# A state-space layer with experts on one core: first projections from centred input, finer layer-norm steps, and two products between two sets of transposes

## The chip, the cores and the metric

The kernel runs on one core of a Trainium2 chip. The metric is device time in microseconds of one execution; the median of several runs is given. Five engines work side by side, each with its own instruction stream in order: TensorE (PE, with weight loads as PEld), VectorE (DVE), ScalarE (ACT), GpSimd (POOL), and SyncE (SP), whose queue issues all DMAs here. [...]

## The reference, cut to what matters

One sequence of L = 2048 tokens with 1024 channels, all float32. The input is layer-normed; the normed input goes to a Mamba-2 style layer and to a base projection with low-rank experts; both results are added to the input.

```
xn    = (x - mean(x)) / sqrt(var(x) + 1e-5)               # over 1024 channels
proj  = xn @ in_proj_w.T                                  # gate 4096 | x 4096, B 1024, C 1024 | dt 64
xBC   = silu(causal_conv4(proj[x,B,C]) + conv_bias)
dt    = softplus(proj[dt] + dt_bias);  dA = exp(dt * -exp(A_log))
state = state * dA + (dt * x) outer B;  y = state @ C     # per token, 64 heads, 8 groups
y     = y + D * x;  yn = rmsnorm_per_group(y) * norm_weight * silu(gate)
attn  = yn @ out_proj_w.T
ffn   = xn @ W_base.T + b_base + lora(top-2 of 8 experts of rank 16, from xn)
out   = x + attn + ffn
```

## The kernel before, in words

Channels lie on partitions, tokens along the free axis. The sequence is cut into two halves `s` of 1024 tokens (`TS`), each into two blocks of 512 (`TB`), each into chunks of 128 (`Q`).

**The large products** are done in pairs of 128-row weight tiles by a seven-product scheme (`pair`). A product is four matmuls of 128x512 in the program, which the trace shows as eight records. Products go round PSUM tiles `pa`, `px`, `py` of the pool `ps_proj`. The seven left operands are four weight quarters `a11, a12, a21, a22` loaded by DMA and four sums `s1..s4` made on GpSimd (line 395) and stored to DRAM for the second half (line 397). The loads of the left operands are issued in the order a11, a21, a22, store of s1, store of s2, a12, store of s3, store of s4. The seven right operands `ops_of["x", s]` are the normed input's quarters `b11, b21, b22` and four differences (`t1, t2, t4`, and `b22 - b12` in the place of b12). Within a pair DVE adds `s16` (line 448) and `s15` (line 452) out of PSUM, and evicts two of the four results with an addition (line 494); ACT copies `s1` (line 444) and evicts another with an activation (line 492). Product 7 goes into the same PSUM tile as product 6 and must wait until s16 has read it; product 4 likewise waits until the eviction after product 7.

**The first pair** cannot use differences that do not exist yet, so `plain_pair` does its four results straight: each is eight matmuls of 128x512 of weights by normed quarters, evicted by ACT.

**A start in pieces.** The first half is layer-normed in four pieces of 256 tokens (`ln_first`): mean over channels by matmuls with ones, subtraction on DVE, squares on ACT, variance by matmuls with ones, square root on ACT, reciprocal and multiplication on DVE into the operands. `small_first` then makes dt, router and low-rank products (`sm`) of two 128-token chunks a time. The order on PE is written out by hand from line 850 on: variances of pieces 0 and 1, `small_first(0)`, the mean of piece 2, `small_first(1)`, the mean of piece 3, and then the products of the plain pair with the rest between them.

**The main loop** goes over 32 blocks (half, group, block of 512) and in each over four chunks `c`: one such step is called a slot here. A slot takes `n` products from the stream (4 or 5, from a plan of due numbers), and between them the work of the scan: `scan_b` of this chunk (`ps_y`, `ps_e`, `ps_st`), and `scan_a` of the following one in three steps: (1) DVE scans the decays into `es` (line 673); (2) PE multiplies B by C and transposes B into one PSUM bank, "aux" (`ps_cb`), ACT copies both out (`cbm` line 683, `bt` line 685), DVE multiplies `es` by `cbm` into `dab` (line 687); (3) PE transposes x into the same bank (`ps_xt`), ACT scales it into `xdt` (line 698), GpSimd makes `xdd` (line 704). The bank has one buffer, so `ps_xt` has to wait for the copy `bt`. The root mean square of a finished block (`ps_nv`, evicted at line 797) uses that bank too, in slot c = 0.

```python
            products(1, parts[1])
            products(1, parts[2])
            next(a, None)          # step 2: B by C, transpose of B
            products(1, parts[3])
            next(a, None)          # step 3: transposes of x
```

`parts` holds side steps: the next block's convolution (`conv`, slots c = 1 and 2), gating of the block before (`norm_gate`, c = 0), squares (`norm_squares`, c = 3), and pieces of the small chain (`small`). In blocks 2, 5, 8 and 11 there is also `ln_next`, which norms a piece of the second half for its operands; the stages of those pieces stand in slots c = 1, 2 and 3, and in the block that follows come the steps of `small` for it. PE's order is as written; a scheduler orders the other engines' instructions when the kernel is built.

**The end** is the output projection, again in pairs, with accumulation in SBUF.

Of the kernel before, what the change touches and what calls it, by code (L numbers as in the profile page):

```python
# [27 lines left out]
P = 128  # L28
# [14 lines left out]
def mamba_lora_kernel(  # L43
# [125 lines left out]
    def over_channels(of, bank, name):  # L169
        ps = ps_one.tile([P, 2 * Q], F32, tag=bank, name=f"ps_{name}")  # L170
        for k, part in enumerate(of):
            mm(ps, ones, part, start=(k == 0), stop=(k == len(of) - 1))
        return ps

    def ln_first(i):


        flat = piece_of[0, i].rearrange("p k n q -> p k (n q)")
        bank = ("aux", "y", "e", "st")[i]
        if i < 2:  # L180
            of = [flat[:, k, :] for k in range(KT)]
        else:
            of = halved(flat, f"0_{i}")
        ps = over_channels(of, bank, f"mean_0_{i}")
        mean = p2.tile([P, 2 * Q], F32, tag="state", name=f"mean_0_{i}")
        nc.scalar.activation(mean, ps, AF.Copy, scale=1.0 / DM)
        sqs = []
        for h in range(2):
            normal(flat[:, 4 * h : 4 * h + 4, :], mean, ALU.subtract)
            for k in (4 * h, 4 * h + 2):  # L190
                sq = ev.tile([P, 2, 2 * Q], F32, tag="ev", name=f"lsq_0_{i}_{k}")
                nc.scalar.activation(sq, flat[:, k : k + 2, :], AF.Square)
                sqs.append(sq)
        if i < 2:
            of = [sqs[k // 2][:, k % 2, :] for k in range(KT)]
        else:
            of = pairs_sum(sqs)
        yield
        ps = over_channels(of, bank, f"var_0_{i}")
        std = p1.tile([P, 2 * Q], F32, tag="xdd", name=f"std_0_{i}")  # L200
        nc.scalar.activation(std, ps, AF.Sqrt, bias=eps, scale=1.0 / DM)
        nc.vector.reciprocal(std, std)
        cols = slice((i % 2) * 2 * Q, (i % 2 + 1) * 2 * Q)
        for h, j in enumerate((0, 1) if i < 2 else (6, 2)):
            normal(flat[:, 4 * h : 4 * h + 4, :], std, ALU.mult, ops_of["x", 0][j][:, :, cols])
        yield

    def first_sums():


        b11, b21, b22, t4, t1, t2, b12 = ops_of["x", 0]
        nc.vector.tensor_tensor(t1, b12, b11, ALU.subtract)
        nc.vector.tensor_tensor(t2, b22, t1, ALU.subtract)
        nc.vector.tensor_tensor(t4, b21, t2, ALU.subtract)
        yield
        nc.vector.tensor_tensor(b12, b22, b12, ALU.subtract)
        yield

    def ln_next(s, i):

        t = piece_of[s, i]
        flat = t.rearrange("p k n q -> p k (n q)")

        of = halved(flat, f"{s}_{i}")
        yield
        ps = over_channels(of, "st", f"mean_{s}_{i}")
        mean = p2.tile([P, 2 * Q], F32, tag="lnst", name=f"mean_{s}_{i}")
        nc.scalar.activation(mean, ps, AF.Copy, scale=1.0 / DM)
        yield
        sqs = []  # L230
        for h in range(2):
            normal(flat[:, 4 * h : 4 * h + 4, :], mean, ALU.subtract)
            for k in (4 * h, 4 * h + 2):
                sq = ev.tile([P, 2, 2 * Q], F32, tag="ev", name=f"lsq_{s}_{i}_{k}")
                nc.scalar.activation(sq, flat[:, k : k + 2, :], AF.Square)
                sqs.append(sq)
        of = pairs_sum(sqs)
        yield
        ps = over_channels(of, "st", f"var_{s}_{i}")
        std = p2.tile([P, 2 * Q], F32, tag="lnst", name=f"std_{s}_{i}")  # L240
        nc.scalar.activation(std, ps, AF.Sqrt, bias=eps, scale=1.0 / DM)
        nc.vector.reciprocal(std, std)
        for h in range(2):
            normal(flat[:, 4 * h : 4 * h + 4, :], std, ALU.mult)
        yield
        b11, b12 = t[:, 0:KH, 0, :], t[:, 0:KH, 1, :]
        b21, b22 = t[:, KH:KT, 0, :], t[:, KH:KT, 1, :]
        cols = slice(i * Q, (i + 1) * Q)
        t4, t1, t2, t3 = (
            ev.tile([P, KH, Q], F32, tag="ev", name=f"t_{s}_{i}_{j}") for j in range(4)  # L250
        )
        nc.vector.tensor_tensor(t1, b12, b11, ALU.subtract)
        nc.vector.tensor_tensor(t2, b22, t1, ALU.subtract)
        nc.vector.tensor_tensor(t4, b21, t2, ALU.subtract)
        nc.vector.tensor_tensor(t3, b22, b12, ALU.subtract)
        for j, src in enumerate((b11, b21, b22, t4, t1, t2, t3)):
            nc.sync.dma_start(xop_d[j][:, :, cols], src)
        yield
# [205 lines left out]
        quarter(1, 0, px, s1)  # L464
        yield

    def plain_pair(key, name, quarters, ops, quarter):


        t = left_operands(key, quarters, True)  # L470
        w = [t[i] for i in ("a11", "a12", "a21", "a22")]
        yield
        b11, b21, b22, _, _, _, b12 = ops()
        for n, (lo, hi) in enumerate(((b11, b21), (b12, b22))):
            for m in range(2):
                ps = ps_proj.tile([P, TB], F32, tag="proj", name=f"ps_p_{name}")
                for h, b in enumerate((lo, hi)):
                    for k in range(KH):
                        mm(
                            ps, w[2 * m + h][:, k, :], b[:, k, :],  # L480
                            start=(h + k == 0), stop=(h + k == KH), skip_group_check=True,
                        )
                quarter(m, n, ps, None)
                yield

    def stored(to, first_tile, s, func):


        def quarter(m, n, ps, add):
            e = ev.tile([P, TB], F32, tag="ev", name="ev")  # L490
            if add is None:
                nc.scalar.activation(e, ps, func)
            else:
                nc.vector.tensor_tensor(e, ps, add, ALU.add)  # L494
                if func != AF.Copy:
                    nc.scalar.activation(e, e, func)
            at = s * TS + n * TB
            nc.sync.dma_start(to[:, first_tile + m, at : at + TB], e)

        return quarter  # L500
# [24 lines left out]
    def in_pairs():  # L525
        for s in range(NS):
            ops = lambda s=s: ops_of["x", s]
            for g in range(G):
                if s and g == 0:
                    load_ops(s)  # L530
                for q, (i0, i1) in enumerate(((0, 1), (2, 3), (4, 5))):
                    tis = [4 * g + i if i < 4 else 32 + 8 * (i - 4) + g for i in (i0, i1)]
                    args = (
                        f"x{g}_{q}", f"x_{s}_{g}_{q}", halves(*(w_in[32 + t] for t in tis)), ops,
                        stored(raw_d[g], i0, s, AF.Copy),
                    )
                    yield pair(*args, s == 0) if s + g + q else plain_pair(*args)
                for q in range(2):
                    t = 4 * g + 2 * q
                    yield pair(  # L540
                        f"g{g}_{q}", f"g_{s}_{g}_{q}", halves(w_in[t], w_in[t + 1]), ops,
                        stored(gate_d[g], 2 * q, s, AF.Silu), s == 0,
                    )
            for q in range(4):
                yield pair(
                    f"b{q}", f"b_{s}_{q}", halves(w_base[2 * q], w_base[2 * q + 1]), ops,
                    stored(base_d, 2 * q, s, AF.Copy), s == 0,
                )
# [298 lines left out]
    next(lns[1])  # L847
    next(lns[0])
    next(lns[1])
    small_first(0)  # L850
    next(lns[2])
    small_first(1)
    next(lns[3])
    next(lns[2])
    next(stream)
    next(lns[3])
    next(stream)
    small_first(2)
    small_first(3)
    op_sums = first_sums()  # L860
    next(op_sums)
    next(stream)
    next(stream)
    next(op_sums)
    home = {
        "dtp": (p2, "xdt"), "u": (p2, "ecp"), "u2": (p2, "ecp"), "po": (p2, "xdt"),
        "at": (p2, "ecp"), "ex": (p1, "xdd"), "da": (p1, "es"), "run": (p2, "dab"),
# [35 lines left out]
    for b, blk in enumerate(blocks):  # L903
# [8 lines left out]
        for c in range(NQ):  # L912
# [8 lines left out]
                load_piece(*piece, "sg", p1)  # L921
                ln = ln_next(*piece)
            if after == 0 and c == 2:
                next(ln)
            if after == 0 and c == 3:
                side += steps(ln, 1)
            if after == 1 and c in (0, 2, 3):
                side += steps(rest, 1)
            if c in (1, 2) and nxt:
# [19 lines left out]
            if c == NQ - 1:  # L949
                sq = norm_squares(*blk)  # L950
                parts[1] += steps(sq, 2)
                parts[2] += steps(sq, 1)
            products(1, parts[1])
            products(1, parts[2])
            next(a, None)
            products(1, parts[3])
            next(a, None)
            if after == 0 and c in (1, 2):
                next(ln)
            for i in range(4, n):  # L960
                products(1, parts[i])

            if after == 0 and c == 1:
                next(ln)
# [153 lines left out]
```

## Time and profile before

| what | value |
|---|---|
| median of 3 runs | 3573.68 us (3573.0 to 3574.63) |
| the profiled execution's own time | 3579.01 us |
| its span, first to last instruction | 3577.2 us |
| PE busy | 3514.0 us (98%) |
| DVE, ACT, POOL busy | 2322.4, 943.7, 685.6 us |
| mean granted TensorE clock | 0.995 |

The span is 1.8 us short of that execution's time. The execution lay 5.3 us above the median of the runs. A row of the timeline has: start, duration, engine, line, operation, output and inputs, shapes, how many were merged, and in brackets the idle time before it and who ended it. A row of the windows has the stretch, its length, the busy time of PE, PEld, DVE, ACT and POOL (with numbers of instructions), the granted clock, the DMA share and GB/s. A row of the waits has the waiting operation, what it waited for, the sum in us, how many times, and the longest.

### The profile page before, as it was taken

The page shows a single profiled execution, that of the slowest core. Times are in us where ns is not written, and L with a number is a line of the kernel's source. Part 1 is how long each engine was busy: PE and PEld are TensorE (multiplying, and loading weights), DVE is VectorE, ACT ScalarE, POOL GpSimd, SP SyncE. Part 2 cuts the span into 40 slices and gives each one's busy share as a digit, 9 for nine tenths or more (in the row PEclk, how much of TensorE's full clock was granted, in tenths as well). Part 3 has the DMA queues.
Part 4 walks back from the last instruction along what each step waited for, and adds up shares of the span by engine and source line. Part 5 has one row for each costly group of instructions (what it writes and reads, how often), then busy time and mean ns, then how long its engine had stood idle before and what let it go on. Part 6 is the DMA issues. An engine that isn't in the chain of part 4 may idle for free. (4 is left out here: it accounts for less than half of the span.)

```text
span 3577.2 us, 36348 instructions
## 1 busy us (share of the span) xinstructions
PE 3514.0 (98%) x12370; PEld 1731.0 (48%) x12370; DVE 2322.4 (65%) x2713; ACT 943.7 (26%) x2170; POOL 685.6 (19%) x503
## 2 busy tenths in 40 slices
PE   8999999999999999999999999999999999999999
PEld 6444444544544444455455455455455444444444
DVE  6537877877877777676766777766776544434432
ACT  2213343333333333233333333333332100000000
POOL 2223323333323322011111111111112202220000
PEclk9999999999999999999999999999999999999999
DMA  3546565656555567656565555565656564455432
GB/s 124 183 154 205 187 199 186 193 191 197 179 189 185 182 195 244 207 191 189 182 195 176 184 184 194 180 192 183 184 188 208 207 209 160 135 165 196 151 112 88
DMA packets 394681, 648.60 MB, mean 181 GB/s; under 512 B 33024, under 2 KB 129408, under 8 KB 393600
## 3 DMA queue, kind: packets, MB, share of 16 engines
q1 hardware_dynamic: 394496, 646.27, 55.9%
q8 instruction: 99, 1.62, 0.2%
q14 instruction: 86, 0.70, 0.1%
HBM read 433.28 MB, written 212.86 MB: 181 GB/s over the span
## 5 line engine op out<-in xcount | busy, mean ns | idle before, releaser
L673 DVE TENSOR_TENSOR_SCAN es<-dab,here 128x1024 f32<-128x1024 f32 x128 | 304.9, 2382 | 347.0 <-POOL xdd L704 342.8
L704 POOL TENSOR_TENSOR xdd<-xdt,es 128x512 f32<-128x512 f32 x128 | 143.9, 1124 | 1212.1 <-ACT xdt L698 1005.6
L76 PE MATMUL ps_x_x<-op,s_x 128*128 128x512 f32 x752 | 340.7, 596 | 0.0
L76 PE MATMUL ps_y_x<-op,s_x 128*128 128x512 f32 x752 | 338.8, 593 | 0.0
L76 PE MATMUL ps_a_x<-op,a_x 128*128 128x512 f32 x752 | 338.1, 592 | 0.0
L632 DVE SCALAR_TENSOR_TENSOR xg<-rawx,cw,xg 128x512 f32<-128x512 f32 x384 | 295.4, 815 | 13.7 <-ACT xg L626 12.7
L698 ACT ACTIVATE xdt<-ps_xt,dt 128x64 f32<-128x64 f32 x1024 | 225.2, 331 | 189.3 <-PE ps_xt L79 187.5
L76 PE MATMUL ps_y_g<-op,s_g 128*128 128x512 f32 x512 | 232.0, 596 | 1.6 <-DVE s_g L452 1.6
L76 PE MATMUL ps_x_g<-op,s_g 128*128 128x512 f32 x512 | 231.8, 596 | 0.0
L76 PE MATMUL ps_x_o<-yop,s_o 128*128 128x512 f32 x512 | 230.2, 592 | 1.1 <-DVE s_o L448 1.1
L76 PE MATMUL ps_a_o<-yop,a_o 128*128 128x512 f32 x512 | 230.3, 592 | 0.0
L76 PE MATMUL ps_a_g<-op,a_g 128*128 128x512 f32 x512 | 230.2, 592 | 0.0
L76 PE MATMUL ps_y_o<-yop,s_o 128*128 128x512 f32 x512 | 230.2, 592 | 0.0
L76 PEld LDWEIGHTS ps_a_x<-op,a_x 128*128 128x128 f32 x752 | 140.3, 190 | 162.8 <-issue 162.1
L76 PEld LDWEIGHTS ps_x_x<-op,s_x 128*128 128x128 f32 x752 | 140.7, 191 | 161.4 <-issue 160.4
L757 POOL TENSOR_TENSOR state<-state,tot 128x512 f32<-128x512 f32 x112 | 159.3, 1423 | 304.6 <-PE ps_e L76 280.4
L76 PEld LDWEIGHTS ps_y_x<-op,s_x 128*128 128x128 f32 x752 | 139.2, 190 | 157.5 <-issue 155.0
L444 ACT COPY s_o<-ps_a_o 128x512 f32<-128x512 f32 x32 | 18.8, 586 | 707.5 <-PE ps_a_o L76 627.3
L687 DVE TENSOR_TENSOR dab<-es,cbm 128x1024 f32<-128x1024 f32 x128 | 164.2, 1283 | 30.3 <-ACT cbm L683 29.7
L76 PE MATMUL ps_x_x<-op,a_x 128*128 128x512 f32 x376 | 171.3, 599 | 9.2 <-DVE ev L494 9.1
L632 DVE SCALAR_TENSOR_TENSOR bc<-rawb,cw,bc 128x512 f32<-128x512 f32 x192 | 163.5, 884 | 12.7 <-ACT bc L626 12.4
L76 PEld LDWEIGHTS ps_y<-dab,xdt 128*64 128x64 f32 x2048 | 117.8, 136 | 102.3 <-issue 56.1
(213 smaller groups left out, 5030.0 us busy)
## 6 DMA issues: line engine op xcount, KB each, us to landing
dab<-da_d SPq DMA_DIRECT2D x128, 512.0 KB, 4.8
raw<-ev SPq DMA_DIRECT2D x192, 256.0 KB, 2.8
a_x<-in_w_in_dram SPq DMA_DIRECT2D x168, 256.0 KB, 3.4
ecp<-run_d SPq DMA_DIRECT2D x256, 128.0 KB, 3.6
gate<-ev SPq DMA_DIRECT2D x128, 256.0 KB, 3.0
sg<-gate SPq DMA_DIRECT2D x32, 1024.0 KB, 6.1
y<-xg SPq DMA_DIRECT2D x64, 512.0 KB, 3.6
yop<-y SPq DMA_DIRECT2D x32, 1024.0 KB, 6.2
```

The source lines that it names most:

```text
L76: tc.keep_in_program_order(nc.tensor.matmul(*args, **kw))
L444: nc.scalar.copy(s1, pa)
L632: nc.vector.scalar_tensor_tensor(dst[:, i, :], raw[:, i, k : k + TB], cw[:, ti, k : k + 1], dst[:, i, :], ALU.mult, ALU.add,)
L673: nc.vector.tensor_tensor_scan(es.rearrange("p h t -> p (h t)"), dab.rearrange("p h t -> p (h t)"), here, 0.0, ALU.mult, ALU.add,)
L687: nc.vector.tensor_tensor(ms, es, cbm.unsqueeze(1).to_broadcast([P, HG, Q]), ALU.mult)
L698: nc.scalar.activation(xdt[:, h, :], x_t[:, h, :], AF.Copy, scale=dt_of[s][:, half * NQ + c, at : at + 1],)
L704: nc.gpsimd.tensor_tensor(xdd, xdt, es[:, :, Q - 1 : Q].to_broadcast([P, HG, HP]), ALU.mult)
L757: nc.gpsimd.tensor_tensor(s3, s3, tot_of[s][:, half * NQ + c, hs].unsqueeze(2).to_broadcast([P, HG, HP]), ALU.mult,)
```

## The change

Three parts. In the start, `plain_pair` takes the centred pieces (x minus its mean) in place of the normed operands, a piece of 256 tokens at a time, so that a result is sixteen matmuls of 128x256; DVE multiplies by 1/sqrt(var+eps) (`rstd`) as it evicts. Its first two products stand right after the variances of pieces 0 and 1, each followed by the mean of piece 2 or 3; the small products come after them, and the four differences of the operands are made in one go. In `ln_next`, the work is cut into more steps, and these are spread over the slots: centring and squares move from ahead of slot c = 2 into its side steps, the variance to the end of that slot, the multiplications into slot c = 3. In every slot, step 2 of `scan_a` moves ahead of one more product, so that two products stand between it and the transposes of x.

```diff
 def ln_first(i):
-        std = p1.tile([P, 2 * Q], F32, tag="xdd", name=f"std_0_{i}")
+        cols = slice((i % 2) * 2 * Q, (i % 2 + 1) * 2 * Q)
+        if i % 2 == 0:
+            rstd_of[i // 2] = p2.tile([P, TB], F32, tag="xdt", name=f"rstd_{i // 2}")
+        std = rstd_of[i // 2][:, cols]
         nc.scalar.activation(std, ps, AF.Sqrt, bias=eps, scale=1.0 / DM)
         nc.vector.reciprocal(std, std)
...
 def first_sums():
         nc.vector.tensor_tensor(t4, b21, t2, ALU.subtract)
-        yield
         nc.vector.tensor_tensor(b12, b22, b12, ALU.subtract)
-        yield
...
 def ln_next(s, i):
                 sqs.append(sq)
-        of = pairs_sum(sqs)
-        yield
-        ps = over_channels(of, "st", f"var_{s}_{i}")
+            nc.vector.tensor_tensor(sqs[2 * h], sqs[2 * h], sqs[2 * h + 1], ALU.add)
+            if h:
+                nc.vector.tensor_tensor(sqs[0], sqs[0], sqs[2], ALU.add)
+            yield
+        ps = over_channels([sqs[0][:, 0, :], sqs[0][:, 1, :]], "st", f"var_{s}_{i}")
...
         nc.vector.reciprocal(std, std)
+        yield
         for h in range(2):
             normal(flat[:, 4 * h : 4 * h + 4, :], std, ALU.mult)
-        yield
+            yield
...
         nc.vector.tensor_tensor(t2, b22, t1, ALU.subtract)
+        yield
         nc.vector.tensor_tensor(t4, b21, t2, ALU.subtract)
...
-    def plain_pair(key, name, quarters, ops, quarter):
+    def plain_pair(key, name, quarters, quarter):
         t = left_operands(key, quarters, True)
-        w = [t[i] for i in ("a11", "a12", "a21", "a22")]
-        yield
-        b11, b21, b22, _, _, _, b12 = ops()
-        for n, (lo, hi) in enumerate(((b11, b21), (b12, b22))):
+        yield
+        for n in range(2):
             for m in range(2):
-                ps = ps_proj.tile([P, TB], F32, tag="proj", name=f"ps_p_{name}")
-                for h, b in enumerate((lo, hi)):
-                    for k in range(KH):
+                ps = ps_proj.tile([P, 2, 2 * Q], F32, tag="proj", name=f"ps_p_{name}")
+                for i in range(2):
+                    x = piece_of[0, 2 * n + i].rearrange("p k n q -> p k (n q)")
+                    for k in range(KT):
+                        w = t[f"a{m + 1}{k // KH + 1}"]
                         mm(
-                            ps, w[2 * m + h][:, k, :], b[:, k, :],
-                            start=(h + k == 0), stop=(h + k == KH), skip_group_check=True,
+                            ps[:, i, :], w[:, k % KH, :], x[:, k, :],
+                            start=(i + k == 0), stop=(k == KT - 1), skip_group_check=True,
                         )
-                quarter(m, n, ps, None)
+                quarter(m, n, ps.rearrange("p a t -> p (a t)"), rstd_of[n], ALU.mult)
...
 the written-out start:
     next(lns[1])
+    next(stream)
+    next(lns[2])
+    next(stream)
+    next(lns[3])
     small_first(0)
     next(lns[2])
     small_first(1)
     next(lns[3])
-    next(lns[2])
-    next(stream)
-    next(lns[3])
     next(stream)
     small_first(2)
+    next(stream)
     small_first(3)
-    op_sums = first_sums()
-    next(op_sums)
-    next(stream)
-    next(stream)
-    next(op_sums)
+    first_sums()
...
 the main loop:
             if after == 0 and c == 2:
-                next(ln)
+                side += steps(ln, 2)
             if after == 0 and c == 3:
-                side += steps(ln, 1)
+                side += steps(ln, 4)
...
             products(1, parts[1])
+            next(a, None)
             products(1, parts[2])
-            next(a, None)
             products(1, parts[3])
             next(a, None)
-            if after == 0 and c in (1, 2):
+            if after == 0 and c == 1:
                 next(ln)
             for i in range(4, n):
                 products(1, parts[i])
+            if after == 0 and c == 2:
+                next(ln)
```

More of the change, by code (lines that the diff above doesn't have):

```diff
@@ L173, in over_channels @@
         return ps
+    rstd_of = {}
     def ln_first(i):
@@ L199, in ln_first @@
         ps = over_channels(of, bank, f"var_0_{i}")
-        std = p1.tile([P, 2 * Q], F32, tag="xdd", name=f"std_0_{i}")
+        cols = slice((i % 2) * 2 * Q, (i % 2 + 1) * 2 * Q)
+        if i % 2 == 0:
+            rstd_of[i // 2] = p2.tile([P, TB], F32, tag="xdt", name=f"rstd_{i // 2}")
+        std = rstd_of[i // 2][:, cols]
         nc.scalar.activation(std, ps, AF.Sqrt, bias=eps, scale=1.0 / DM)
         nc.vector.reciprocal(std, std)
-        cols = slice((i % 2) * 2 * Q, (i % 2 + 1) * 2 * Q)
         for h, j in enumerate((0, 1) if i < 2 else (6, 2)):
@@ L465, in pair, with quarter @@
         yield
-    def plain_pair(key, name, quarters, ops, quarter):
+    def plain_pair(key, name, quarters, quarter):
         t = left_operands(key, quarters, True)
-        w = [t[i] for i in ("a11", "a12", "a21", "a22")]
         yield
-        b11, b21, b22, _, _, _, b12 = ops()
-        for n, (lo, hi) in enumerate(((b11, b21), (b12, b22))):
+        for n in range(2):
             for m in range(2):
-                ps = ps_proj.tile([P, TB], F32, tag="proj", name=f"ps_p_{name}")
-                for h, b in enumerate((lo, hi)):
-                    for k in range(KH):
-                        mm(
-                            ps, w[2 * m + h][:, k, :], b[:, k, :],
-                            start=(h + k == 0), stop=(h + k == KH), skip_group_check=True,
+                ps = ps_proj.tile([P, 2, 2 * Q], F32, tag="proj", name=f"ps_p_{name}")
[3 more added lines that the diff above has]
+                        w = t[f"a{m + 1}{k // KH + 1}"]
+                        mm(
+                            ps[:, i, :], w[:, k % KH, :], x[:, k, :],
+                            start=(i + k == 0), stop=(k == KT - 1), skip_group_check=True,
                         )
-                quarter(m, n, ps, None)
+                quarter(m, n, ps.rearrange("p a t -> p (a t)"), rstd_of[n], ALU.mult)
                 yield
     def stored(to, first_tile, s, func):
-        def quarter(m, n, ps, add):
+        def quarter(m, n, ps, add, alu=ALU.add):
             e = ev.tile([P, TB], F32, tag="ev", name="ev")
@@ L493, in quarter @@
             else:
-                nc.vector.tensor_tensor(e, ps, add, ALU.add)
+                nc.vector.tensor_tensor(e, ps, add, alu)
                 if func != AF.Copy:
@@ L532, in in_pairs @@
                     tis = [4 * g + i if i < 4 else 32 + 8 * (i - 4) + g for i in (i0, i1)]
[L533 to L537, printed above, removed]
+                    key, name = f"x{g}_{q}", f"x_{s}_{g}_{q}"
+                    quarters = halves(*(w_in[32 + t] for t in tis))
+                    to = stored(raw_d[g], i0, s, AF.Copy)
+                    if s + g + q:
+                        yield pair(key, name, quarters, ops, to, s == 0)
+                    else:
+                        yield plain_pair(key, name, quarters, to)
                 for q in range(2):
```

## The prediction, made before the changed kernel was run

> **What bounds the kernel now.** I read the page first: PE is busy 3514.0 us of a span of 3577.2, so all that can be won without removing matmuls is 63 us of gaps, and what a slow clock adds to the matmuls. Then the windows by stage, to see where the gaps lie, and the waits of PE, to see who ends them.
>
> ```profile
> 0.00:92.00 92.00, 75.67 (x274) 55.21 (x275) 60.13 (x69) 24.68 (x44) 19.49 (x33) 0.93 0.37 123
> 400.00:1320.00 920.00, 887.81 (x3403) 449.38 (x3402) 710.29 (x880) 325.57 (x727) 270.46 (x193) 0.99 0.59 191
> 1320.00:2400.00 1080.00, 1077.57 (x4264) 540.41 (x4263) 761.28 (x867) 361.92 (x866) 155.84 (x113) 1.00 0.60 192
> ...
> PE ps_xt L79 <- ACT bt L685: 14.7, 7, 5.5
> PE ps_x_g L76 <- DVE ev L494: 9.5, 4, 4.5
> PE ps_x_x L76 <- DVE ev L494: 9.1, 4, 4.8
> PE ps_sm L76 <- ACT std L201: 6.6, 1, 6.6
> PE ps_mean L76 <- DVE half L166: 4.7, 1, 4.7
> ```
>
> The start lacks 16.3 us of PE, the stretch with the second half's layer-norm pieces and their small chains (400 to 1320) lacks 32.2, all the rest 14.7. Each part of the change aims at one row of the waits. Then the timeline of the start, PE, SP and POOL:
>
> ```profile
> 13.74 7.07 PE L76 MATMUL ps_var<-lsq,ones 128*128 128x256 f32 x32
> 27.43 8.35 PE L76 MATMUL ps_sm<-wsm,op 128*128 128x200 f32 x32 [6.62 <-ACT std L201]
> 47.43 2.05 PE L76 MATMUL ps_mean<-half,ones 128*128 128x256 f32 x4 [4.70 <-DVE half L166]
> 91.32 3.60 PE L76 MATMUL ps_a_x<-op,a_x 128*128 128x512 f32 x8
> ...
> 17.77 1.28 SPq L391 DMA_DIRECT2D a_x<-in_w_in_dram  x3
> 27.05 0.42 SPq L391 DMA_DIRECT2D a_x<-in_w_in_dram  x1
> ...
> 30.25 1.30 POOL L395 TENSOR_TENSOR s_x<-a_x,s_x 128x512 f32<-128x512 f32 x1 [1.82 <-DMA a_x<-in_w_in_dram]
> ```
>
> The reader is to see that the quarter a12 of the first pair is issued only at 27.05, behind the stores of s1 and s2, which wait for GpSimd, and lands at 30.25.
>
> **Part 1, the start.** The work of PE hardly changes: four products of 32 records at 0.221 us (the variances: 7.07 / 32) are 7.07 us each, against 6.87 before (13.90 us for two, less overlap). Weights take 0.19 us a record and stay hidden. DVE gains four evictions of 0.68 us, ACT loses four of 0.60. The question is when each can run, so I walk it in the new order.
>
> Variances end at 20.8. a11 lands at about 21.2 (17.77 plus the median 3.4 from issue to landing); four matmuls with it take 1.7 us; the next needs a12. PE then stands from 22.9 to 30.25: the gap that ended at 27.43 now ends 2.8 us later. The clock is granted in steps of 3.4 us, and after such a gap at half speed:
>
> ```profile
> 28.00:32.00 4.00, 4.00 (x14) 4.00 (x13) 3.97 (x3) 0.00 (x0) 1.72 (x2) 0.50 0.71 221
> 170.00:172.00 2.00, 2.00 (x4) 0.83 (x3) 2.00 (x3) 0.00 (x0) 0.53 (x1) 0.50 0.66 245
> ```
>
> Twelve more matmuls take 5.2 us, or 8.2 with some 6 us at half speed: 38.4. DVE's queue has the eviction of this product ahead of the three sums for the mean of piece 2 (0.7 + 2.0 us), so PE waits to 41.5 for that mean (0.9 us), then does the second product to 49.3. Again eviction and three sums: PE waits to 52.3 for the mean of piece 3. From there nothing is late: that mean (0.9), four pairs of small products (10.99 us for two pairs, so 22.0), variances 2 and 3 (0.9 each) and two products (13.8) come to 38.5, so the second pair starts at about 90.8, and at 92.5 if the gap before 52.3 also halves the clock for one step. Before: 91.32. Behind it, the small chain on DVE starts with the second pair instead of at 78.14, after the fourth difference (2.29 us). It held DVE for 22 us; now s16, s15 and the eviction after product 7 stand inside it. That eviction is about 21 to 23 us behind the pair's start, and product 4 wants it after 6 x 3.43 = 20.6: 0.2 to 2.4 us of waiting. The chain's result is due on PE 27 us after that start and is ready at about 25. So the start is worth 92.5 - 91.3 and about 1 us of that wait, **+2 us (slower)**, with bounds of -5 (no half speed, no DVE wait) and +5. SP's stores of the four results move with them, ahead of a store and loads for the third pair, which is not due for 24 us; POOL's sums keep their place.
>
> [...] But the row 170 to 172 shows half speed after a gap of only 2.15 us (with another of 1.65 us some 4 us before it). [...] I take the row.
>
> **Part 3, two products before the transposes of x.** The worst of the seven waits:
>
> ```profile
> 1024.72 3.60 PE L76 MATMUL ps_a_x<-op,a_x 128*128 128x512 f32 x8
> 1031.05 0.68 DVE L448 TENSOR_TENSOR s_x<-ps_x_x,s_x 128x512 f32<-128x512 f32 x1
> 1032.42 1.06 ACT L638 ACTIVATE xg<-xg 128x1024 f32<-128x1024 f32 x1 [5.31 <-DVE xg L632]
> 1033.53 0.27 ACT L685 COPY bt<-ps_cb 128x128 f32<-128x128 f32 x1
> 1033.85 1.11 PE L79 MATMUL ps_xt<-ident,xg 128*128 128x128 f32 x4 [5.53 <-ACT bt L685]
> ```
>
> ACT stands in the convolution's silu, which waits for DVE; bt is behind it. In the new order bt is ahead of that silu. But what is late next is s16 on DVE, for product 7: with the same DVE work ahead of it, it ends at about 1032.4, so PE resumes then instead of 1034.76: 2.3 won, not 5.5. So went through all: at 582.71 0.85 (next product needs only ACT's copy); at 933.36 0.4 of 1.03 (s15, behind the moved dab of 1.23); at 1207.13 1.4; at 1251.12 about 1.1 of 3.01 (one of two squares of the norm still ahead of bt); at 1281.60 nothing of 2.28, since DVE has no gap from 1276 to 1304 and PE waits for it at 1303.48 anyway; at 199.09 nothing (that scan is written without products between). Sum 6.1. Half-speed steps fall away for about 2.5 us (one of two at 1033, half of one at 1251).
>
> It also adds waits. dab (1.23 us, 128 times) now stands ahead of the eviction of one more product, and B by C asks for the bank one product earlier: against the root mean square's eviction that leaves -1.2 us at 556.8, -0.4 at 1000.3 and 0.5 or more elsewhere. Bank 1.6; at 1007.60 0.5; other evictions I put at 1.5. The trace before cannot show those: bounds 0 and 8. After 1320 PE waits 2.4 us in 1080, so DVE's slack is the cover there; were it gone, each slot would cost up to 1.2.
>
> **Part 2, finer layer-norm.** DVE's 14 us a piece stay; slot c = 2 loses some 4.5 us of it and c = 3 gains it. But the eight waits for ev lie mostly in the block after a piece, where the small chain, the gating (reciprocal 3.35, product 2.29) and the convolution meet. At 473.73 (4.54) DVE is held by the gate's DMA, whose buffer is the piece's, freed as late as before. The wait at 755.98 (4.77) shrinks, since the new order puts ev behind three convolution steps, not six (3 x 0.74 = 2.2), and with it one half-speed step (1.7): 3.9 won. I cost the rest at nothing, bounds -5 and +3; the seven stores a piece keep their place.
>
> **Sum.** +2.0 - 6.1 - 2.5 - 3.9 + 1.6 + 0.5 + 1.5 = -6.9 us. Made against the profiled execution (3579.0), taken over to the median of the runs: 3573.7 - 6.9 = **3567**.
>
> **The rivals.** (a) *All the waits go.* For it: the releaser in each row is just what the change moves. Against it: DVE's next piece of work is late by nearly as much. It would give 14.1 (transposes) + 6.4 (half-speed steps at 1033, 1251, 1282) and 5 in the start: 3548. (b) *DVE in order becomes the bound: slower.* The moved dab holds the eviction of the second product by 1.23 us in each of some 60 slots of the first half. It decides once those evictions have less than 1.23 us to spare against the reuse of their PSUM tile two products later. DVE was busy 710 of 920 us there and eight such waits exist already; if one slot in five pays 1 us (12), nothing is won at the transposes beyond that, and the start costs 5: 3573.7 - 6 + 12 + 5 = 3585. (c) *The waits only change their names*, DVE setting the pace throughout: 3574.
>
> **How the numbers follow.** Forecast case 0.55 (3560 to 3575), (a) 0.15, (b) 0.22, (c) 0.08. The runs of this kernel tell some 0.2% from no change, 7.1 us. Half of the forecast case lies below 3566.6, half within: faster 0.42, same 0.36, slower 0.22. As both signs have a share, the range goes to both rivals: 3548 to 3585.
>
> **What would show it.** Right: PE idle to about 30.2 in the start, ended by the DMA of a_x; two gaps of about 3 us before ps_mean; the second pair starting between 88 and 93; ps_xt waiting for bt below 4 us in all; the wait at the block after the first piece still 4 us or more; new waits for s_x and ev. Wrong: the second pair starting before 86, or waits of PE for DVE above 30 us in all, or waits in the second half of the scan.

## The result, and the profile after

| | before | changed |
|---|---|---|
| median, run by run on one chip | 3574.63 us (7 runs, 3573.0 to 3576.93) | 3562.27 us (7 runs, 3560.46 to 3564.31) |
| ratio | | 0.9965, 95% interval 0.9953 to 0.9977 |
| profiled execution, its own time | 3579.01 us | 3561.65 us |
| its span | 3577.2 us | 3559.9 us |
| PE busy | 3514.0 us | 3503.0 us |

The change saves 12.4 us by the medians, where 6.9 was forecast. Measured once more in another series it gave 0.9974 (0.9965 to 0.9983). First the windows of the changed kernel by stage, with the columns of the windows shown before:

```profile
0.00:92.00 92.00, 73.67 (x332) 64.84 (x333) 46.44 (x45) 20.17 (x36) 17.54 (x33) 0.93 0.39 129
400.00:1320.00 920.00, 893.54 (x3431) 452.58 (x3430) 710.28 (x885) 326.64 (x734) 272.71 (x193) 0.99 0.59 192
1320.00:2400.00 1080.00, 1079.45 (x4300) 540.64 (x4299) 764.99 (x872) 360.02 (x862) 153.19 (x114) 1.00 0.61 194
```

The start lacks 18.3 us of PE (16.3 before), the stretch to 1320 us 26.5 (32.2), the stretch behind it 0.55 (2.4). Then the waits of PE:

```profile
PE ps_x_g L76 <- DVE ev L501: 13.6, 4, 6.0
PE ps_mean L76 <- DVE half L166: 7.1, 3, 3.5
PE ps_da L79 <- ACT xdt L707: 6.8, 3, 3.9
PE ps_p_x L76 <- DVE op L148: 6.7, 1, 6.7
...
PE ps_x_x L76 <- DVE ev L501: 3.1, 3, 2.6
PE ps_y_g L76 <- DVE s_g L458: 2.7, 2, 1.6
PE ps_x_x L76 <- DVE s_x L454: 2.3, 1, 2.3
PE ps_cb L76 <- ACT rms L806: 1.2, 1, 1.2
...
PE ps_y L76 <- ACT xdt L707: 0.6, 3, 0.2
...
PE ps_xt L79 <- ACT bt L694: 0.5, 1, 0.5
```

The 14.7 us of `ps_xt<-bt` are down to 0.5. In their place stand `ps_da<-xdt` (6.8, from 1.2), `s_x` (2.3, from none), `s_g` (2.7, from 1.6) and `rms` (1.2): 10.2 us of the 14.2 are back under other names. `ev` as a whole went from 18.6 to 16.7. By the rows of waits the change would be worth only a few microseconds: the idle time of PE fell by 6.3 us (63.2 to 56.9). Its busy time fell by 11.0. The start, with PE, SP's queue and POOL:

```profile
20.91 1.97 PE L76 MATMUL ps_p_x<-piece,a_x 128*128 128x256 f32 x8 [0.58 <-DMA a_x<-in_w_in_dram]
29.54 8.35 PE L76 MATMUL ps_p_x<-piece,a_x 128*128 128x256 f32 x24 [6.67 <-DVE op L148]
41.42 1.23 PE L76 MATMUL ps_mean<-half,ones 128*128 128x256 f32 x4 [3.52 <-DVE half L166]
42.44 8.70 PE L76 MATMUL ps_p_x<-piece,a_x 128*128 128x256 f32 x32
53.85 1.13 PE L76 MATMUL ps_mean<-half,ones 128*128 128x256 f32 x4 [2.71 <-DVE half L166]
92.69 3.60 PE L76 MATMUL ps_a_x<-op,a_x 128*128 128x512 f32 x8
...
26.44 0.42 SPq L397 DMA_DIRECT2D a_x<-in_w_in_dram  x1
...
29.54 1.26 POOL L401 TENSOR_TENSOR s_x<-a_x,s_x 128x512 f32<-128x512 f32 x1 [1.20 <-DMA a_x<-in_w_in_dram]
```

The row at 29.54 names DVE, but POOL, which needs a12, resumes at the very same instant on the DMA issued at 26.44: PE waits for a12. (A second profile of the same kernel puts the same wait, 6.65 us, down to the DMA of `a_x`.) And the place of the worst of the seven waits:

```profile
1023.39 3.60 PE L76 MATMUL ps_a_x<-op,a_x 128*128 128x512 f32 x8
1026.82 0.60 PE L79 MATMUL ps_xt<-ident,xg 128*128 128x128 f32 x4
1029.71 3.70 PE L76 MATMUL ps_x_x<-op,s_x 128*128 128x512 f32 x8 [2.29 <-DVE s_x L454]
1034.71 0.41 PE L79 MATMUL ps_da<-ident,ex 128*64 128x128 f32 x2 [1.08 <-ACT xdt L707]
```

Where 5.53 us stood, s16 is late next with 2.29, and 1.08 more goes to a wait for the bank.

**What the waits do not show.** The order of the work on PE lets the two kernels be laid side by side at each chunk's first `ps_y`. In the profiles the changed kernel is 10.1 us ahead at 1315 us, and 17.3 at 2789. So 7 us come from a stretch in which the waits of before add up to 3.2 us, all of them in one row:

```profile
PE ps_y L76 <- ACT xdt L698: 3.2, 12, 0.6
```

There, a slot of before on PE:

```profile
2149.48 0.60 PE L79 MATMUL ps_xt<-ident,xg 128*128 128x128 f32 x4
2149.92 3.60 PE L76 MATMUL ps_x_g<-op,a_g 128*128 128x512 f32 x8
2153.98 1.76 PE L76 MATMUL ps_y<-dab,xdt 128*64 128x128 f32 x15 [0.46 <-ACT xdt L698]
```

and ScalarE in it, also before:

```profile
2152.15 1.06 ACT L638 ACTIVATE bc<-bc 128x1024 f32<-128x1024 f32 x1 [1.83 <-DVE bc L632]
2153.11 0.61 ACT L496 ACTIVATE ev<-ev 128x512 f32<-128x512 f32 x1
2153.64 1.73 ACT L698 ACTIVATE xdt<-ps_xt,dt 128x64 f32<-128x64 f32 x8
```

The eight copies of `xdt` start only behind these two. The same slot of the changed kernel, PE and then ScalarE:

```profile
2136.90 3.60 PE L76 MATMUL ps_x_g<-op,a_g 128*128 128x512 f32 x8
2140.43 1.13 PE L76 MATMUL ps_y<-dab,xdt 128*64 128x128 f32 x15
...
2140.07 1.11 ACT L707 ACTIVATE xdt<-ps_xt,dt 128x64 f32<-128x64 f32 x5
2141.05 1.08 ACT L647 ACTIVATE bc<-bc 128x1024 f32<-128x1024 f32 x1
```

In the first, 15 small matmuls take 1.76 us: each pair of them needs one of the copies of `xdt`, and they follow ScalarE copy by copy. Only the 0.46 ahead of the first counts as idle; the other 0.67 is counted as busy PE. In the second, the silu of `bc` stands behind the copies and the same 15 take 1.13. Before has 12 such long groups after 1320 us (8.0 us above 1.09 each, and 3.2 of gaps), the changed kernel 7 (4.2 and 0.6): 6.4 of the 7.2 us. (An expectation below says 11; the one at 1560.84 was missed.) In before five of the twelve follow a silu of `bc` that stands ahead of the copies, seven one of `xg`; the seven of the changed kernel all follow one of `xg`. Counted over all slots after 1320 us, a silu starts between the transposes of x and the last of their copies 8 times for `bc` and 16 times for `xg` in before, never for `bc` and 16 times for `xg` in the changed kernel.

### The profile page after: what moved, and what is told of

Read it like the earlier page. It is cut to its first block, busy times and chain, and to the rows that moved or that the text cites. A ratio compares the mean times of both kernels' runs of the same rounds, so it can differ in the third digit from the quotient of the medians.

```text
span 3559.9 us, 36490 instructions
## 1 busy us (share of the span) xinstructions
PE 3503.0 (98%) x12434; PEld 1735.9 (49%) x12434; DVE 2318.1 (65%) x2717; ACT 939.0 (26%) x2166; POOL 676.0 (19%) x503
## 4 chain that ended last, share of the span: by engine, by line
PE 69%; DVE 1%; issue 1%; DMA 0%; ACT 0%; POOL 0%; ACTq 0%; DVEq 0%
PE ps_x_o L76 9%; PE ps_x_x L76 8%; PE ps_a_o L76 6%; PE ps_y_o L76 6%; PE ps_x_g L76 6%; PE ps_y_x L76 5%; PE ps_a_x L76 5%; PE ps_a_g L76 4%; PE ps_y_g L76 4%; PE ps_y L76 3%; PE ps_st L76 2%; PE ps_x_b L76 2%; PE ps_e L76 2%; PE ps_y_b L76 2%; PE ps_a_b L76 2%; PE ps_xt L79 1%
## 5 line engine op out<-in xcount | busy, mean ns | idle before, releaser
L641 DVE SCALAR_TENSOR_TENSOR xg<-rawx,cw,xg 128x512 f32<-128x512 f32 x384 | 298.3, 821 | 11.1 <-ACT xg L635 10.1
```

The lines of the kernel that those rows point to most:

```text
L641: nc.vector.scalar_tensor_tensor(dst[:, i, :], raw[:, i, k : k + TB], cw[:, ti, k : k + 1], dst[:, i, :], ALU.mult, ALU.add,)
```

## The experiments

Two lengths are used below: from the start of the span to the 51st chunk's `ps_y` (**first stretch**, 1314.9 us before) and from there to the 127th's (**second stretch**, 1474.0). Executions of one and the same order differ by some microseconds in the first: before has 1314.9 us, e5, which has the old order in all blocks of that stretch, 1305.0. So the 10.1 us above cannot be read as what the change wins there. In the second they differ less: 1471.7 to 1474.0 in four profiles of the old order, 1466.8 and 1467.1 in two of the changed kernel. What a change makes in microseconds is worked out as (1 - ratio) x the median of before in the same series.

| run | what it is | ratio, 95% interval |
|---|---|---|
| e1_order | part 3 alone | 0.9976, 0.9965 to 0.9986 |
| e2_start | part 1 alone | 1.0001, 0.9992 to 1.0009 |
| e3_ln | part 2 alone | 1.0004, 0.9996 to 1.0012 |
| e4_ln_order | parts 2 and 3 | 0.9970, 0.9959 to 0.9982 |
| e5_order_late | part 3 in blocks 13 to 31 | 0.9982, 0.9974 to 0.9990 |
| e6_order_early | part 3 in blocks 0 to 12 | 0.9982, 0.9975 to 0.9990 |
| e7_silu_behind | before, silu of bc behind the copies | 0.9963, 0.9949 to 0.9976 |
| e8_a12_second | changed, a12 loaded second | 0.9953, 0.9940 to 0.9965 |
| e9_changed_again | changed | 0.9974, 0.9965 to 0.9983 |
| e10_silu_pair | changed, both silus behind | 0.9934, 0.9921 to 0.9946 |
| e11_silu_a12 | e10 and a12 second | 0.9912, 0.9899 to 0.9926 |
| e12_silu_a12_means | e11 and means first | 0.9947, 0.9935 to 0.9959 |

**The order alone.**

```diff
             products(1, parts[1])
+            next(a, None)
             products(1, parts[2])
-            next(a, None)
             products(1, parts[3])
```

> The kernel before with the third part alone: the product of B with C, its two copies and the product of es into dab come one product earlier, so two products stand between them and the transposes of x. Times against the kernel before (3574.6). Theory O (the order change carries most of the gain of 12.4 us): -8 to -13 us, the rows ps_xt<-bt fall from 14.7 us to below 1 us, and the work between 1007 and 1303 us and in the second half of the scan comes earlier by some 10 us in all. Rival L (the finer layer-norm carries it): -1 to -5 us, as the forecast's sum for this part with its returned waits had it (-5.0). Rival J (only both parts together win, because each alone leaves the vector engine late in the block after a piece): -3 us or less, and the rows ps_xt<-bt come back under the name s_x or ev with about the same sum.

Measured: -8.6 us (-12.5 to -5.0); the second stretch is 1467.4 us against 1474.0. The waits of PE:

```profile
PE ps_x_g L76 <- DVE ev L494: 12.7, 4, 6.0
...
PE ps_da L79 <- ACT xdt L698: 6.7, 3, 3.8
...
PE ps_x_x L76 <- DVE s_x L448: 2.3, 1, 2.3
PE ps_cb L76 <- ACT rms L797: 2.1, 2, 1.2
...
PE ps_xt L79 <- ACT bt L685: 0.5, 1, 0.5
```

Theory O holds by the time. Of the new waits that J named only `s_x` came; `ev` as a whole fell from 18.6 to 13.7. `da` and `rms`, which no theory named, are this part's doing.

**The start alone**: part 1 as in the diff above, the rest as before.

> The kernel before with the first part alone: first pair from the centred x, standard deviation multiplied in at the eviction, new order of the start. Theory (forecast, and the trace of the whole change, where the second pair starts 1.4 us later): +0.5 to +2.5 us against the kernel before, second pair starting at 92 to 93.5 us of the span, all later work shifted by as much. Rival (the start gains something that shows only later, because the small chain and the evictions on the vector engine leave it earlier): -2 to -6 us, with the rows at 200 and 315 us earlier than before by 2 us or more.

Measured: +0.4 us (-2.9 to +3.2); the second pair starts at 92.17 us. The rival's -2 to -6 is met only at the edge of the interval. The rows that it named stand at 197.5 and 313.1 us, 1.6 ahead of before's profile, but the six other profiles with the old start have them at 194.6 to 196.4 and 310.1 to 312.0, so nothing leaves the start earlier. By the time, +2 cannot be told from nothing.

**The layer-norm alone**: part 2 as in the diff above, the rest as before.

> The kernel before with the second part alone: the layer-norm of a piece of the second half in ten steps, two of them beside the products of slot 2 and four beside those of slot 3. Theory O: -2 to -5 us, mostly the wait at 756 us (4.77 us before) and one step of half clock with it; the rows ps_xt<-bt stay near 14.7 us. Rival L: -7 to -12 us, with the waits at 1208, 1251 and 1282 us smaller as well. Rival J: 0 to -2 us.

Measured: +1.4 us (-1.4 to +4.3). The part costed at -3.9 gives nothing that can be measured. The wait near 756 us fell from 4.77 to 3.2, not by the 2.2 of the forecast, a step of half clock stays there (the product behind that wait takes 5.37 us, the next ones 3.60), and the row `ps_x_g<-ev` grew from 9.5 to 12.1. L is out; J is the nearest.

**Both.**

> The second and the third part together, with the start of the kernel before. Theory (parts add): the whole change's -12.4 us less the start's +1.4, so -13 to -15 us, and the sum of the two parts run alone within 2 us. Rival J: this sum is more than 4 us larger than that of the two parts alone. Rival (the start gives something): -9 us or less.

Measured: -10.7 us (-14.6 to -6.4), against -7.2 for the sum of the two alone. The difference of 3.5 lies within the intervals, so whether the layer-norm helps once the order is changed stays open. The value lies between the theory's -13 to -15 and the rival's -9 or less, and its interval reaches into both; J's 4 us is not reached.

**The order in one half of the blocks.** Here `next(a, None)` stands at its new place only where the block's number satisfies a condition, b > 12 or b <= 12:

```diff
+            if (b > 12):
+                next(a, None)
             products(1, parts[2])
-            next(a, None)
+            if not (b > 12):
+                next(a, None)
             products(1, parts[3])
```

> The kernel before with the order change only in blocks 13 to 31 of the scan (from about 1330 us on). There the trace of before shows no wait of PE worth naming, but 11 groups ps_y<-dab,xdt of 15 matmuls that take 1.76 us in place of 1.09, and 3.0 us of gaps ahead of them: PE follows ScalarE's eight copies of xdt one by one, which stand behind the silu of bc. Theory S (these stretched groups are what the order change wins): -4.5 to -6.5 us against the kernel before, 7 long groups or fewer left, the stretch from 1330 to 2790 us shorter by 5 to 6.5 us. Rival F (the seven waits ps_xt<-bt of the first half carry the gain of 8.3 us): 0 to -2.5 us.

Measured: -6.4 us (-9.3 to -3.6). The second stretch is 1468.0 us, with 7 long groups; all seven waits `ps_xt<-bt` are still there (15.2 us). Rival F, that those waits carry the whole gain, is out.

> The kernel before with the order change only in blocks 0 to 12 of the scan (to about 1330 us), where all seven waits ps_xt<-bt lie. Theory S: -1 to -4 us (what is left of the 8.3 us); the rows ps_xt<-bt go, but the waits for ev at 474 and 1290 us and three waits ps_da<-xdt grow by nearly as much; the stretch after 1330 us is as long as before. Rival F: -6 us or more.

Measured: -6.4 us (-8.9 to -3.6). The second stretch is 1472.9 us, as in the old order. Theory S had the rows right (`ps_xt<-bt` at 0.5, `ps_x_g<-ev` 12.4, `ps_da<-xdt` 6.8) but put the gain too low, and F's number is met here: the first half of the order change is worth about as much as the second. The two halves sum to -12.8, the whole part was measured at -8.6 (-12.5 to -5.0), so the halves are known to some 3 us each.

**The silu behind the copies, in the old order.** On ScalarE alone, an edge of issue order puts the silu of `bc` behind the last copy of `xdt` of its slot; its emission moves two convolution steps later:

```diff
-                if i % 2:
+                if dst is xg and i == 1:
+                    if last_xdt:
+                        with tc.issue_after(last_xdt[-1]):
+                            nc.scalar.activation(bc, bc, AF.Silu)
...
+                if dst is xg and i % 2:
```

> The kernel before, no order change; only the silu of bc on ScalarE is queued behind the eight copies of xdt of its slot. Theory S: -3 to -6 us, the long groups ps_y after 1330 us fall from 11 or 12 to 7 or fewer, while the rows ps_xt<-bt of the first half keep 5 us or more. Rival (it is the moved product of B with C, the bank or dab, and not the silu, that shortens the second half): -1 to +2 us, with 11 or 12 long groups left.

Measured: -13.2 us (-18.2 to -8.6), as much as the whole change. The second stretch is 1467.0 us, just what the order change makes of it; 9 long groups are left (7 or fewer were expected), with gaps of 0.1 us or less ahead of them. No silu of `bc` stands ahead of the copies any more; that of `xg` still does in 16 slots. Yet the waits for `bt` in the first half are still there:

```profile
PE ps_xt L79 <- ACT bt L693: 13.7, 4, 5.5
PE ps_x_g L76 <- DVE ev L494: 8.6, 4, 4.9
```

So the second half can be won without moving B by C, the bank or `dab`: the place of one silu in ScalarE's queue is enough. The gain is larger than theory S had it. That these two rows and `ps_x_x<-ev` (6.2, from 9.1) are 4.8 us smaller than in before is part of it; the rest of the difference is not placed. ScalarE also loads its tables 90 times here, not 95 (1.28 us each); four of those five fall in the first stretch, where no run tells their share from that of the order of work.

**The start's load.**

```diff
         load("a11", q11)
+        if key == "x0_0":
+            load("a12", q12)
         if fresh:
             load("a21", q21)
```

(and not again behind s2)

> The changed kernel with the quarter a12 of the first pair loaded right behind a11, ahead of a21, a22 and the stores of s1 and s2. Theory D (forecast: the load's place holds the start): a12 lands at 21 to 23 us in place of 29.5, the gap of 6.7 us ahead of the second half of the first product falls below 1.5 us, the second pair starts 3 to 7 us earlier than 92.7, and the time is 3 to 7 us below that of the changed kernel, so 15 to 19 us below the kernel before. Rival V (the vector engine sets the pace of the start, since the sums for the means and the evictions follow each other there): the second pair starts within 1.5 us of 92.7, time 10 to 13 us below the kernel before.

Measured: 16.8 us below before (12.5 to 21.4), 4.3 more than the changed kernel in its first series and 7.5 more than in its second. The start:

```profile
20.44 7.07 PE L76 MATMUL ps_p_x<-piece,a_x 128*128 128x256 f32 x32
33.30 2.07 PE L76 MATMUL ps_mean<-half,ones 128*128 128x256 f32 x4 [5.78 <-DVE half L166]
35.16 9.19 PE L76 MATMUL ps_p_x<-piece,a_x 128*128 128x256 f32 x32
47.06 1.13 PE L76 MATMUL ps_mean<-half,ones 128*128 128x256 f32 x4 [2.71 <-DVE half L166]
...
85.91 3.60 PE L76 MATMUL ps_a_x<-op,a_x 128*128 128x512 f32 x8
```

The gap of 6.67 is gone, and the second pair starts 6.8 us earlier. Theory D holds; DVE takes some of it back (the wait for `half` goes from 3.52 to 5.78).

**The last series**: the changed kernel again, and three kernels built on it. In e10 the silu of `bc` and the second silu of `xg` get the edge of e7, and each convolution takes two steps more; e11 adds the early a12; e12 adds the new place of the means:

```diff
     next(lns[1])
+    next(lns[2])
+    next(lns[3])
     next(stream)
-    next(lns[2])
     next(stream)
-    next(lns[3])
     small_first(0)
```

> The changed kernel once more, beside three kernels built on it, on the same chip. All theories: 8 to 15 us below the kernel before; the sum of its parts run alone (order -8.6, layer-norm +1, start 0) and its first measurement (-12.4) lie in that span.

Measured: -9.3 us (-12.5 to -6.1).

> The changed kernel with both silus of the convolution that can stand ahead of the copies of xdt (that of bc and the second of xg) queued behind the copies of their slot. Theory S (ScalarE's queue ahead of the copies is what stretches ps_y after 1330 us): the 7 long groups left (4.2 us, and 0.6 us of gaps) go, -3 to -5 us against the changed kernel. Rival R (the silu's reader, the next block's B by C and transposes, is late instead): -1 to +3 us, with new waits of ps_cb or ps_xt for bc or xg.

Measured: 3546.79 us (3546.23 to 3547.88) beside 3562.04 (3559.43 to 3564.1) for the changed kernel, -15.3 us by the medians. No long group and no silu ahead of the copies is left, and the second stretch is 1460.6 us against 1467.1: 6.5. The other 9 or so come in the first stretch, and here the rows show in part where:

```profile
PE ps_x_g L76 <- DVE ev L501: 13.1, 4, 6.0
...
PE ps_da L79 <- ACT xdt L723: 2.3, 1, 2.3
PE ps_y_g L76 <- DVE s_g L458: 1.6, 2, 1.2
```

`ps_da<-xdt` fell from 6.7 to 2.3, `ps_cb<-rms` from 1.2 to none, a wait `ps_mean<-half` of 0.8 near 1201 us to none: 6.4 of the 9. `ps_da` goes into the bank that the copies of `xdt` empty, so what holds the copies on ScalarE holds PE there too. In the changed kernel of this series:

```profile
504.81 1.06 ACT L647 ACTIVATE xg<-xg 128x1024 f32<-128x1024 f32 x1 [3.62 <-DVE xg L641]
505.77 0.50 ACT L707 ACTIVATE xdt<-ps_xt,dt 128x64 f32<-128x64 f32 x2
```

The last copy ends at 508.0, and `ps_da` starts at 508.1 after a wait of 1.83. The order change had made this worse: up to 1320 us a silu of `xg` stands ahead of the copies in 3 slots of before, in 7 of the changed kernel, in none of e10. The other two rows that are smaller are not the edit's doing: `s_x` is 0.5 here and 2.3 in the changed kernel, but also 0.5 in e4 and e8 without the edit and 2.3 in e11 and e12 with it, and `s_g`, 1.6 here, is 1.8 in e4 without the edit. The three profiles with 0.5 have a step of half clock at about 1000 us (in e10 the product at 999.84 takes 5.14 us, behind a gap of 2.55; others take 3.60), the six with 2.3 have none: PE then reaches the place later and waits 1.8 us less for DVE, so a half-clock step there costs next to nothing. ScalarE's table loads fall from 95 to 92, all three in the first stretch. Both theories put the gain too low; R's new waits are not there.

> Both: the two silus behind the copies, and a12 loaded right behind a11. Theory (the two add): -7 to -10 us against the changed kernel, the second pair starting at about 86 us as in the run with a12 alone.

Measured: 3539.05 us (3537.51 to 3541.44), -23.0 us against the changed kernel; the second pair starts at 86.00. The two parts add: a12 gives 7.7 us on top of e10, where the second pair starts at 93.62. (The expectation of -7 to -10 was too small because e10's was.) It is the fastest version, 0.9912 (0.9899 to 0.9926) of before.

> As the one before, and the sums for the means of pieces 2 and 3 issued ahead of the first product's eviction. Theory D (in the start PE waits twice for the sum half behind an eviction on the vector engine): the two waits ps_mean<-half of 5.8 and 2.7 us shrink to below 2 us together, -3 to -6 us against the kernel without this. Rival (the evictions, now behind all sums of both pieces, hold the PSUM tiles and the later products): -1 to +3 us, and new waits of ps_p_x for ev.

Measured: 3551.52 us, 12.5 slower than e11. The start:

```profile
28.81 2.07 PE L76 MATMUL ps_mean<-half,ones 128*128 128x256 f32 x4 [7.94 <-DVE half L166]
41.56 2.08 PE L76 MATMUL ps_mean<-half,ones 128*128 128x256 f32 x4 [10.68 <-DVE half L166]
43.42 15.68 PE L76 MATMUL ps_p_x<-piece,a_x 128*128 128x256 f32 x64
```

The rival has the sign, not the mechanism: PE does not wait for an eviction. The means stand ahead of both products in PE's order too, and PE idles 18.6 us for the sums. The eviction was not what had to go from between; the product is the cover.

## Why the prediction was right, and where it was not

**Sign and size.** -6.9 was forecast for the whole, -12.4 and -9.3 were measured. That the total lies so near is in part luck, as the places show. To place the gain, the first stretch is set against the runs. A profiled execution can lie off its kernel's median; since the second stretch hardly varies, the offset is taken from the first. In the old order of the first 13 blocks (before, e2, e3, e5) this gives, as an estimate, 1310.5, 1309.2, 1307.2 and 1309.3 us; with the order change (e1, e4, e6) 1303.2, 1301.6 and 1303.6; the whole change 1305.3 and 1304.8. The second stretch is 1471.7 to 1474.0 in the old order (before, e2, e3, e6) and 1466.8 to 1468.0 in the new (e1, e4, e5, and the changed kernel twice). The medians of before themselves lie up to 4.9 us apart from series to series (3569.69 to 3574.63), which is not taken out, so the figures of the first stretch are good to a few microseconds only. By the means, the whole change wins about 4 us in the first stretch, where -6.9 was forecast, and 5.6 in the second, where nothing was.

**The start** was right step by step up to the second pair: PE idle to 29.5 (forecast 30.25), the mean of piece 2 at 41.4 (41.5), that of piece 3 at 53.9 (52.3), the second pair at 92.69 (92.5). The last agreement is partly luck: the half-clock step that was booked behind the second gap came behind the first. The wait of 0.2 to 2.4 us inside that pair did not come: PE has no gap from 92.69 to 122.33 us. The sign of the +2 is borne out by the profiles: the second pair starts at 88.9 to 91.3 us in the seven with the old start, at 92.2 to 93.6 in the four with the new one and the old load (3.1 us later by the means). In the time of the whole kernel e2 does not show it.

**The row.** The row 170 to 172 was taken: a gap of 3 us may bring half speed. After the gap of 3.52 the clock was granted at half for one step of 3.41 us (42.31 to 45.72), after that of 2.71 it was not, and two gaps of 1.57 and 2.11 some 4 us apart (164 to 172 us) brought none, where nearly the same pair (1.65 and 2.15) did in before, for 3.41 us from 169.40 on. So the row does not foretell one gap, and from what length on a gap brings half speed is not shown.

**Part 3 in the first half** was right in kind: went to nearly nothing at the transposes, s16 late next at 1029.71, the bank's wait for `rms` 1.2 at 556.84 as worked out, nothing won near 1282 (7.1 us of waits there, 4.8 before). A term was missing: `ps_da`, 6.8 us in three waits (1.2 in one before). It was left out because only the bank's neighbour `ps_cb` was asked for its reader; the small chain's transposes use that bank too. The bounds for "other evictions", 0 to 8, were wide enough to hold it.

**Part 3 in the second half** is the step that failed: "After 1320 PE waits 2.4 us in 1080". That is idle time, not what the waits cost. 8.0 us more, by 2789 us, lay inside groups counted as busy. e5 shows it (-6.4 with the order changed only there); e7 and e10 show the cause, the silus ahead of the copies.

**Part 2** failed in its one gain: "the wait at 755.98 (4.77) shrinks". In the changed kernel it does (0.18), but in e6, with the order change and no part 2, it is 0.17; and 15 us later stands `ps_da<-xdt` with 3.87 and a step of half clock (3.41 us from 769.35 on in the changed kernel). Alone, the part leaves 3.21 there and measures +1.4.

**The rivals.** (c), waits that change their names, describes most of the first half's rows. (b), DVE in order, did not decide: no eviction in the second half made PE wait. Of the signs named for a wrong forecast, "above 30 us" of waits for DVE is met at 36.6 as the rows are printed, and not at 29.9 once the 6.7 that belongs to a12 is taken out.

## What to carry to other kernels

Before a stretch is called free of waits, compare the duration of like groups in it: the matmuls that follow the copies of `xdt` one by one are counted as busy here, and their rows are only longer than their neighbours (1.76 us in place of 1.13). Ask of every bank and tile who else fills it, and of every engine what stands ahead of the copies that PE needs; here the place in ScalarE's queue of two silus of 1.06 us per block was worth 15.3 us, more than the whole change. A load that the first product needs goes ahead of stores that wait for other engines: the early a12 gave 7.7 us on top of e10.

## What was unexpected of the hardware

The time of one and the same kernel varied by several microseconds, 3565.5 to 3575.7 in 29 runs of before in one series. The granted clock shows one reason: in the last series the six runs of before with a mean clock of 0.994 have a median of 3572.45 us, the nine with 0.995 one of 3569.88. Outside the tail, the profile of before has 37.5 us at half clock, in steps of 3.41 us and multiples of it, that of the changed kernel 30.7, e11 17.1. Two profiles of the changed kernel have them at different places in the start (25.2 to 35.5 and 42.3 to 45.7; 25.9 to 32.7 and 39.5 to 46.3). So a half-clock step in a single profile is partly luck, and the forecast's 2.5 us for two of them (1033 and 1251) was worked from one execution: e5, which has the old order there, shows one step of 3.41 at 1026.9, where before has two.
